# A graph layer with eleven instead of eight tiles summed from rows fetched one by one

## The chip, the cores and the metric

The kernel runs on one core of one Trainium2 chip. The metric is the device time of one execution in microseconds (us); the median of three runs before the change is 1190.65 us (1189.58 to 1191.01).

## The reference

There are N = 6250 nodes with 256 features each and E = 200,000 directed edges, sorted by destination. Every node also has an edge to itself. A graph layer comes first, then a feed-forward layer with experts; both are added to their input.

```python
x = x + gnn(layernorm(x), edge_index, W, b, prelu_a)
#   deg  = number of edges into a node (its own included); dinv = rsqrt(deg)
#   h    = x @ W
#   out  = segment_sum(h[src] * dinv[src] * dinv[dst], dst) + b
#   gnn  = where(out > 0, out, prelu_a * out)
x = x + ffn(layernorm(x)[None], Wr, br, W1, b1, W2, b2, gamma, beta)[0]
#   the mean of all rows picks 2 of 8 experts (softmax, capacity, softmax, top 2)
#   y = sum over the two of weight * (gelu(x @ W1 + b1) @ W2 + b2)
#   ffn = layernorm(y + x) * gamma + beta
```

The change lies in the segment sum: for each node, the sum of h * dinv over the sources of its edges.

## The kernel before, in words

Nodes are cut into NT = 49 tiles of 128. Each row of h * dinv is kept as two parts of reduced precision, high and low, side by side: 512 numbers, 2 KB. All 49 tiles of these rows stay in on-chip memory as `hp2`, and a copy of them goes to device memory as `hl_d` (seven stores on SP, line 786). The sum for a tile of destinations is made in one of two ways.

*Dense.* A matrix of edge counts is built, then multiplied with all rows. `one_hots` (line 605) has VectorE compare indices with a list of numbers, once for the low seven bits of the source (`oh_lo`, 128 x 2048) and once for the key that holds the source tile and which of two destinations it is (`oh_key`, 128 x 1568). `counts` (lines 639 and 643) multiplies the two, for each pair of destinations, in a matmul of 98 columns; ScalarE copies four of them at a time into the tile's count matrix `a_t`. `sums` (line 659) then runs 49 matmuls of 512 columns, one per source tile, into the accumulator `po`. A dense tile thus has 64 matmuls of 98 columns and 49 of 512.

*Gathered.* Since edges are sorted by destination, those of one tile are a contiguous piece of the edge list. The kernel takes 36 chunks of 128 edges (GC = 36). `g_edges` (line 704) fetches the piece of the source list and of the destination list, one indirect DMA each per tile, issued by GpSimd (POOL). `fetch` (line 745) issues one indirect DMA per chunk, which brings 128 rows of 2 KB from `hl_d` into one of six buffers `rows`. `g_hot` (lines 759 and 760) has ScalarE make a 128 x 128 matrix per chunk that says which edge goes to which node of the tile, and `g_sums` (lines 769 and 776) adds one matmul of 512 columns per chunk to the accumulator `pg`, after a first one for the edge to itself. `pg` has one buffer.

Eight tiles, the last ones, are gathered (NGT = 8) and 41 are dense (NDT = 41). Both kinds are done in one loop over the dense tiles, each of which is cut into four quarters (QT). Every quarter from the fifth dense tile on (G0 = 4) also holds two chunks of a gathered tile (GQ = 2), so that a gathered tile takes NQ = 18 quarters. The order on PE (TensorE), VectorE, ScalarE, SP and POOL is that of the program text in this part: it is written out by hand (`manual_schedule`), and every engine goes through its own list in order, waiting for what others must have finished. In a quarter the order in the text is: ScalarE's matrices for the chunks, the comparisons for a later quarter, the 16 count matmuls of the next tile with their copies, the 12 or 13 sums of this tile, the steps on finished tiles, and at the end the chunk matmuls and the fetches that refill the buffers they free.

Steps on finished tiles: `node` (lines 673 to 682) copies the accumulator, scales it, adds the bias, applies the slope for negative values, adds the input and stores; `stat` (lines 688 to 696) takes mean and deviation and adds to the running sum `acc` that the choice of experts is made from. `own` (line 651) adds the edge to itself to the count matrix.

`g_check` (lines 711 to 736) runs once, at the end of the third dense tile (`n == G0 - 2`). It subtracts the first node of each gathered tile from all destinations at once (line 711), counts how many fall into their tile, and compares, in a small matmul (line 724), whether the chunks held every edge; `bad_i` then says whether a slow general path is to be run. It uses a `rows` buffer as scratch and the `pg` accumulator. All sixteen list fetches stand ahead of the loop. After the loop the experts are chosen (from line 868 on, the first matmul is line 878) and the feed-forward layer runs.

Of the kernel before, what the change touches and what calls it, by code (L numbers as in the profile page):

```python
# [24 lines left out]
P = 128  # L25
# [9 lines left out]
def gnn_moe_kernel(  # L35
# [59 lines left out]
    QT = 4  # L95
    GC = 36
    GE = GC * P
    GQ = 2
    NQ = GC // GQ
    NGT = (NT - 5) * QT // (NQ + QT)  # L100
    NDT = NT - NGT
    G0 = NDT - 1 - NGT * NQ // QT
    assert E >= GE and GC % GQ == 0 and NQ % 2 == 0 and NQ > QT and G0 >= 4
# [483 lines left out]
    with main:  # L587
# [96 lines left out]
        def stat(n):  # L684
            x1 = x1s.pop(n)
            st = np_.tile([P, 6], F32, name="st2")
            mv = np_.tile([P, 2], F32, name="mv2")
            nc.vector.bn_stats(st, x1)
# [7 lines left out]
            nc.vector.scalar_tensor_tensor(  # L696
                acc[:r], x1[:r], rs[:r], acc[:r], op0=OP.mult, op1=OP.add
            )


        def g_edges():
            for v, t in ((src, g_src), (dst, g_dst)):
                for g in range(NGT):
                    nc.gpsimd.indirect_dma_start(
                        out=t[:, g, :], out_offset=None, in_=v.rearrange("(e o) -> e o", o=1),
                        in_offset=bass.IndirectOffsetOnAxis(ap=g_at[:, g : g + 1], axis=0),
                    )

        def g_check():

            nc.vector.scalar_tensor_tensor(
                g_neg, g_dst, -1.0, g_first.unsqueeze(2).to_broadcast([P, NGT, GC]),
                op0=OP.mult, op1=OP.add,
            )
            some = gp.tile([P, 2 * D], F32R, name="rows").bitcast(F32)[:, : NGT * GC]
            flat = g_neg.rearrange("p g c -> p (g c)")
            nc.vector.tensor_scalar(some, flat, 0.5, None, op0=OP.is_lt)
            nc.vector.scalar_tensor_tensor(
                some, flat, 0.5 - P, some, op0=OP.is_gt, op1=OP.mult
            )  # L720
            nc.vector.tensor_reduce(tot[:, 2:3], some, AX.X, OP.add)
            nc.vector.tensor_tensor(tot[:, 2:3], tot[:, 3:4], tot[:, 2:3], OP.subtract)
            pt = ps_g.tile([P, 2, D], F32, name="pg")[:, 0, :3]
            nc.tensor.matmul(pt, ones, tot[:, :3], start=True, stop=True)
# [15 lines left out]
        def fetch(n):  # L740

            for j in itertools.islice(g_put, n):
                if j < NGT * GC:
                    g_rows[j] = gp.tile([P, 2 * D], F32R, name="rows")
                    nc.gpsimd.indirect_dma_start(  # L745
                        out=g_rows[j], out_offset=None, in_=hl_d,
                        in_offset=bass.IndirectOffsetOnAxis(
                            ap=g_src[:, j // GC, j % GC : j % GC + 1], axis=0
                        ),
                    )  # L750

        def g_hot(j0):

            if not 0 <= j0 < NGT * GC:
                return
            oh = g_hots[j0] = og.tile([P, GQ, P], F32R, name="oh_g")
            for i in range(GQ):
                g, c = divmod(j0 + i, GC)
                nc.scalar.activation(oh[:, i, :], iota_f, AF.Abs, bias=g_neg[:, g, c : c + 1])  # L759
            nc.scalar.activation(oh, oh.bitcast(F32), AF.Relu, scale=-1.0, bias=1.0)  # L760

        def g_sums(j0):
            if not 0 <= j0 < NGT * GC:
                return
            n = NDT + j0 // GC
            if j0 % GC == 0:
# [7 lines left out]
            oh = g_hots.pop(j0)  # L774
            for i in range(GQ):
                nc.tensor.matmul(  # L776
                    pouts[n].rearrange("p k d -> p (k d)"), oh[:, i, :], g_rows.pop(j0 + i),
                    start=False, stop=((j0 + i) % GC == GC - 1),
                )
            fetch(GQ)  # L780

        for n in range(3):
            load(n)
# [8 lines left out]
        for n in ns:  # L792
# [8 lines left out]
            if n in (HK + 6, NT - 1):  # L801
# [4 lines left out]
                for b in range(NBH):  # L806
                    counts(0, (c + 1) * NBH + b)
                one_hots(c + 3) if c == 0 else None
        g_edges()

        assert NHG == QT
        for n in range(NDT):
            for c in range(NHG):
                q = (n - G0) * NHG + c
                g_hot(q * GQ)
# [24 lines left out]
        node(NDT - 1)  # L840
        stat(NDT - 1)
        order.close()

# [426 lines left out]
```

## Time and profile before

| | us |
|---|---|
| median of three runs | 1190.65 |
| the profiled execution | 1190.92 |
| its span | 1189.1 |
| TensorE busy | 1100.9 (93%) |
| VectorE busy | 711.5 (60%) |
| ScalarE busy | 630.9 (53%) |
| GpSimd busy | 529.1 (44%) |
| dense and gathered tiles, about 119 to 788 us of the span | 669 |

Times are measured from the start of the span. PE is TensorE, PEld its weight load, DVE VectorE, ACT ScalarE, POOL GpSimd, SP the engine that issues most of the transfers. A group line gives source line, engine, operation, what is written from what, the shape and a count, then busy time and the mean of one in ns, then the time its engine was idle ahead of it and what ended most of that. A line of an order of time gives start, duration and the same names; in brackets stands idle time ahead of it and what ended it. Matmuls overlap in the pipeline, so the time that one takes is read from the distance of starts.

### The profile page before, as it was taken

How to read it: one execution, taken by the hardware profiler on the slowest of the kernel's cores; microseconds unless marked ns; L12 is line 12 of the kernel's file. 1: busy time of each engine (PE TensorE's matmuls, PEld its weight loads, DVE VectorE, ACT ScalarE, POOL GpSimd, SP SyncE). 2: the span in 40 equal slices, each digit the busy share in tenths (PEclk: the TensorE clock that was granted, in tenths of full speed). 3: DMA queues.
4: the chain of work that ended last, by engine and by line, in shares of the span. 5: the costliest groups of instructions: out<-in, count | busy, mean ns of one | idle time of the engine just before them, and what ended most of it. 6: DMA issues, size and time to landing. Idle time of an engine off the chain costs nothing. (4 is left out here: it accounts for less than half of the span.)

```text
span 1189.1 us, 18227 instructions
## 1 busy us (share of the span) xinstructions
PE 1100.9 (93%) x6706; PEld 842.6 (71%) x6706; DVE 711.5 (60%) x1509; ACT 630.9 (53%) x1547; POOL 529.1 (44%) x526
## 2 busy tenths in 40 slices
PE   7882999999999999999999999952999999999996
PEld 5671878888888888888888888841666666666665
DVE  6759677788787887878878788653222232222222
ACT  3658446666666666666666666611333333333332
POOL 3704703555565555655556555400333333334433
PEclk9895999999999999999999999985999999999998
DMA  8708603565655656556565565504011111111000
GB/s 266 227 12 323 187 27 98 143 155 147 153 141 143 156 146 154 138 143 157 146 154 138 144 157 144 133 23 135 14 42 49 37 36 36 36 36 36 23 18 22
DMA packets 92254, 133.11 MB, mean 112 GB/s; under 512 B 8830, under 2 KB 47390, under 8 KB 92158
## 3 DMA queue, kind: packets, MB, share of 16 engines
q0 software_dynamic: 43584, 80.40, 27.6%
q1 hardware_dynamic: 45266, 49.06, 12.6%
q10 hardware_dynamic: 3308, 2.41, 0.7%
q8 instruction: 54, 0.88, 0.3%
q14 instruction: 42, 0.34, 0.1%
HBM read 104.47 MB, written 27.37 MB: 111 GB/s over the span
## 5 line engine op out<-in xcount | busy, mean ns | idle before, releaser
L659 PE MATMUL po<-hp,a_t 128*128 128x512 f32 x2009 | 504.2, 400 | 0.0
L745 POOL DMA_INDIRECT rows<-hl_d,g_src x288 | 329.2, 1143 | 299.1 <-PE pg L776 228.5
L659 PEld LDWEIGHTS po<-hp,a_t 128*128 128x128 f32 x2009 | 367.1, 189 | 72.7
L643 ACT CAST a_t<-pa 128x392 fp32r<-128x392 f32 x656 | 271.0, 501 | 206.2 <-PE pa L639 204.5
L605 DVE TENSOR_TENSOR oh_lo<-iota,loT 128x2048 bf16<-128x2048 bf16 x164 | 199.5, 1216 | 15.9 <-PE pa L639 15.9
L639 PEld LDWEIGHTS <-oh_lo 128*128 128x128 bf16 x2624 | 128.5, 99 | 68.2 <-issue 25.4
L1200 PE MATMUL p<-xT,w_sb 128*128 128x512 f32 (+1 forms) x416 | 172.6, 573 | 2.5 <-ACT hT L1204 1.8
L639 PE MATMUL pa<-oh_key,oh_lo 128*128 128x98 bf16 x2624 | 153.6, 211 | 22.9 <-DVE oh_key L605 12.3
L1218 PE MATMUL p<-w_sb,hT 128*128 128x256 f32 (+1 forms) x784 | 172.9, 381 | 0.0
L1218 PEld LDWEIGHTS p<-w_sb,hT 128*128 128x128 f32 (+1 forms) x784 | 148.5, 191 | 20.2
L605 DVE TENSOR_TENSOR oh_key<-iota,keyT 128x1568 bf16<-128x1568 bf16 x164 | 158.2, 965 | 0.0
L1200 PEld LDWEIGHTS p<-xT,w_sb 128*128 128x128 f32 x416 | 77.6, 192 | 90.9 <-issue 86.4
L1223 DVE TENSOR_TENSOR yt<-yt,p 128x256 f32<-128x256 f32 (+1 forms) x49 | 20.6, 421 | 164.3 <-PE p L1218 164.3
L1184 POOL TENSOR_TENSOR yt<-yt,b_sb 128x1024 f32<-128x1024 f32 (+1 forms) x13 | 29.1, 2242 | 184.0 <-PE px L1178 124.6
L1204 ACT ACTIVATE hT<-p,b_sb 128x512 f32<-128x512 f32 (+1 forms) x104 | 67.5, 661 | 79.0 <-PE p L1200 78.7
L759 ACT ACTIVATE oh_g<-iota_f,g_dst 128x128 fp32r<-128x128 f32 x288 | 103.8, 425 | 0.0
L776 PE MATMUL pg<-rows,oh_g 128*128 128x512 f32 x288 | 91.1, 397 | 0.0
L1228 ACT ACTIVATE rs<-rs 128x1 f32<-128x1 f32 (+1 forms) x49 | 9.9, 203 | 146.4 <-DVE rs L1227 146.4
L674 DVE TENSOR_TENSOR x<-x,po 128x256 f32<-128x256 f32 x41 | 17.3, 422 | 104.9 <-ACT x L673 104.9
L1233 POOL TENSOR_TENSOR yt<-yt,gamma_bc 128x256 f32<-128x256 f32 (+1 forms) x49 | 35.5, 725 | 90.2 <-DVE yt L1230 90.2
L760 ACT ACTIVATE oh_g<-oh_g 128x256 fp32r<-128x256 f32 x144 | 60.3, 419 | 4.5
L1173 DVE TENSOR_SCALAR yt<-xt,mean,rstd 128x256 f32<-128x256 f32 x49 | 18.8, 444 | 73.0 <-DMA xt<-x_d 72.8
(195 smaller groups left out, 863.3 us busy)
## 6 DMA issues: line engine op xcount, KB each, us to landing
hl_d<-hp SPq DMA_DIRECT2D x7, 1792.0 KB, 10.9
x_d<-x SPq DMA_DIRECT2D x49, 128.0 KB, 1.7
xt<-x_d SPq DMA_DIRECT2D x12, 512.0 KB, 3.9
out_dram<-yt SPq DMA_DIRECT2D x48, 128.0 KB, 1.7
xb<-in_x_dram SPq DMA_DIRECT2D x6, 896.0 KB, 11.9
xs<-in_x_dram SPq DMA_DIRECT2D x41, 128.0 KB, 3.4
rows<-hl_d,g_src POOLq DMA_INDIRECT x288, 3.8
w_sb<-in_L_ffn_W_dram ACTq DMA_DIRECT2D x2, 512.0 KB, 7.8
```

Source lines behind the costliest of these rows:

```text
L605: nc.vector.tensor_tensor(oh, iota2[:, :m, :].unsqueeze(1).to_broadcast([P, HG // 2, m, 2]), v[:, s].rearrange("p (q t) -> p q t", t=2).un ...
L639: nc.tensor.matmul(pa[:, i].rearrange("p j h -> p (j h)"), oh_lo[:, q, :, t], oh_key[:, q, :, t], start=True, stop=True,)
L643: nc.scalar.copy(tiles[n][:, :, b * 2 * BG : (b + 1) * 2 * BG], pa.rearrange("p i j h -> p h (i j)"),)
L659: nc.tensor.matmul(pouts[n].rearrange("p k d -> p (k d)"), tiles[n][:, g, :], hp2[g // TB][:, g % TB].rearrange("p k d -> p (k d)"), start ...
L745: nc.gpsimd.indirect_dma_start(out=g_rows[j], out_offset=None, in_=hl_d, in_offset=bass.IndirectOffsetOnAxis(ap=g_src[:, j // GC, j % GC : ...
L759: nc.scalar.activation(oh[:, i, :], iota_f, AF.Abs, bias=g_neg[:, g, c : c + 1])
L760: nc.scalar.activation(oh, oh.bitcast(F32), AF.Relu, scale=-1.0, bias=1.0)
L776: nc.tensor.matmul(pouts[n].rearrange("p k d -> p (k d)"), oh[:, i, :], g_rows.pop(j0 + i), start=False, stop=((j0 + i) % GC == GC - 1),)
L1200: nc.tensor.matmul(p1[:, :cols], w1_sb[:, e, k, f * P : (f + 1) * P], xT[:, k, :cols], start=(k == 0), stop=(k == ND - 1),)
L1204: nc.scalar.activation(hT[:, e, f, :cols], p1[:, :cols], AF.Gelu, bias=b1_sb[:, e, f : f + 1])
L1218: nc.tensor.matmul(p2[:r], hT[:, e, f, t * P : t * P + r], w2_sb[:, e, f, :], start=(e == 0 and f == 0), stop=(e == TOP_K - 1 and f == NF ...
L1233: nc.gpsimd.tensor_tensor(y, y, gamma_bc[:r], OP.mult)
```

## The change

Eleven tiles are gathered (NGT = 11) and 38 are dense (NDT = 38). A gathered tile takes 13 quarters instead of 18, and its 36 chunks are spread over them as evenly as whole numbers allow: two or three in a quarter, three at most (GM). The chunks begin with the third dense tile (G0 = 2) and end one quarter ahead of the loop's end. Only the edge lists of the first three gathered tiles are fetched ahead of the loop. Those of a later one are fetched in the second quarter of the gathered tile three before it, behind that quarter's row fetches, and the subtraction for it is done eight quarters later (`g_less`). `g_check` no longer does that subtraction, uses other scratch and another accumulator, and stands at the end of dense tile 35, counted from zero. The first six row fetches stand at the end of the second dense tile. The statistics of the last gathered tile come after the loop, behind the last `node`.

```diff
-    GQ = 2
-    NQ = GC // GQ
-    NGT = (NT - 5) * QT // (NQ + QT)
+    NQ = 13
+    NGT = (NT - 2) * QT // (NQ + QT)
     NDT = NT - NGT
-    G0 = NDT - 1 - NGT * NQ // QT
+    G0 = NDT - -(-NGT * NQ // QT)
+    GM = -(-GC // NQ)
...
-        def g_edges():
+        def g_edges(g):
+            if g >= NGT:
+                return
             for v, t in ((src, g_src), (dst, g_dst)):
...
+        def g_less(g):
+            if g >= NGT:
+                return
+            nc.vector.scalar_tensor_tensor(
+                g_neg[:, g, :], g_dst[:, g, :], -1.0,
+                g_first[:, g : g + 1].to_broadcast([P, GC]), op0=OP.mult, op1=OP.add,
+            )
 
         def g_check():
 
-            nc.vector.scalar_tensor_tensor(
-                g_neg, g_dst, -1.0, g_first.unsqueeze(2).to_broadcast([P, NGT, GC]),
-                op0=OP.mult, op1=OP.add,
-            )
-            some = gp.tile([P, 2 * D], F32R, name="rows").bitcast(F32)[:, : NGT * GC]
+            some = sp_.tile([P, D], F32, name="low").bitcast(BF16)[:, : NGT * GC]
...
-            pt = ps_g.tile([P, 2, D], F32, name="pg")[:, 0, :3]
+            pt = ps_o.tile([P, 2, D], F32, name="po")[:, 0, :3]
...
+        def g_chunks(q):
+
+            g, r = divmod(q, NQ)
+            return g, range(r * GC // NQ, (r + 1) * GC // NQ) if 0 <= g < NGT else ()
...
-            fetch(GQ)
+            fetch(len(chunks))
...
-        g_edges()
+        for g in range(3):
+            g_edges(g)
...
-                g_sums(q * GQ)
-            if n == G0 - 2:
+                g_sums(q)
+                if since == 1 and q > 0:
+                    g_edges(q // NQ + 3)
+                if since == 9 and q > 0:
+                    g_less(q // NQ + 3)
+            if n == max(G0 - 2, 1):
+                for g in range(3):
+                    g_less(g)
+                fetch(6)
+            if n == NDT - 3:
                 g_check()
-                fetch(6)
         node(NDT - 1)
+        if since < 2:
+            stat(done)
         stat(NDT - 1)
```

More of the change, by code (lines that the diff above doesn't have):

```diff
@@ L97, in gnn_moe_kernel @@
     GE = GC * P
-    GQ = 2
-    NQ = GC // GQ
-    NGT = (NT - 5) * QT // (NQ + QT)
+    NQ = 13
+    NGT = (NT - 2) * QT // (NQ + QT)
     NDT = NT - NGT
-    G0 = NDT - 1 - NGT * NQ // QT
-    assert E >= GE and GC % GQ == 0 and NQ % 2 == 0 and NQ > QT and G0 >= 4
+    G0 = NDT - -(-NGT * NQ // QT)
+    GM = -(-GC // NQ)
+    assert E >= GE and NQ > QT and G0 >= 2
     const = ctx.enter_context(tc.tile_pool(name="const", bufs=1))
@@ L698, in stat @@
             )
-        def g_edges():
+        def g_edges(g):
+            if g >= NGT:
+                return
             for v, t in ((src, g_src), (dst, g_dst)):
[L703 to L706, printed above, removed]
-                    )
-        def g_check():
-            nc.vector.scalar_tensor_tensor(
-                g_neg, g_dst, -1.0, g_first.unsqueeze(2).to_broadcast([P, NGT, GC]),
-                op0=OP.mult, op1=OP.add,
-            )
-            some = gp.tile([P, 2 * D], F32R, name="rows").bitcast(F32)[:, : NGT * GC]
+                nc.gpsimd.indirect_dma_start(
+                    out=t[:, g, :], out_offset=None, in_=v.rearrange("(e o) -> e o", o=1),
+                    in_offset=bass.IndirectOffsetOnAxis(ap=g_at[:, g : g + 1], axis=0),
+                )
[5 more added lines that the diff above has]
+                g_first[:, g : g + 1].to_broadcast([P, GC]), op0=OP.mult, op1=OP.add,
+            )
+        def g_check():
+            some = sp_.tile([P, D], F32, name="low").bitcast(BF16)[:, : NGT * GC]
             flat = g_neg.rearrange("p g c -> p (g c)")
@@ L750, in fetch, with g_hot, g_sums @@
                     )
-        def g_hot(j0):
-            if not 0 <= j0 < NGT * GC:
+        def g_chunks(q):
+            g, r = divmod(q, NQ)
+            return g, range(r * GC // NQ, (r + 1) * GC // NQ) if 0 <= g < NGT else ()
+        def g_hot(q):
+            g, chunks = g_chunks(q)
+            if not chunks:
                 return
-            oh = g_hots[j0] = og.tile([P, GQ, P], F32R, name="oh_g")
-            for i in range(GQ):
-                g, c = divmod(j0 + i, GC)
+            oh = g_hots[q] = og.tile([P, GM, P], F32R, name="oh_g")
+            for i, c in enumerate(chunks):
                 nc.scalar.activation(oh[:, i, :], iota_f, AF.Abs, bias=g_neg[:, g, c : c + 1])
+            oh = oh[:, : len(chunks), :]
             nc.scalar.activation(oh, oh.bitcast(F32), AF.Relu, scale=-1.0, bias=1.0)
-        def g_sums(j0):
-            if not 0 <= j0 < NGT * GC:
+        def g_sums(q):
+            g, chunks = g_chunks(q)
+            if not chunks:
                 return
-            n = NDT + j0 // GC
-            if j0 % GC == 0:
+            n = NDT + g
+            if chunks[0] == 0:
                 pouts[n] = ps_g.tile([P, 2, D], F32, name="pg")
@@ L773, in g_sums @@
                 )
-            oh = g_hots.pop(j0)
-            for i in range(GQ):
+            oh = g_hots.pop(q)
+            for i, c in enumerate(chunks):
                 nc.tensor.matmul(
-                    pouts[n].rearrange("p k d -> p (k d)"), oh[:, i, :], g_rows.pop(j0 + i),
-                    start=False, stop=((j0 + i) % GC == GC - 1),
+                    pouts[n].rearrange("p k d -> p (k d)"), oh[:, i, :],
+                    g_rows.pop(g * GC + c), start=False, stop=(c == GC - 1),
                 )
-            fetch(GQ)
+            fetch(len(chunks))
         for n in range(3):
@@ L814, in gnn_moe_kernel @@
                 q = (n - G0) * NHG + c
-                g_hot(q * GQ)
+                g_hot(q)
                 one_hots((n + 1) * NHG + c + 1)
```

## The prediction

> **What bounds the kernel now.** I read the 40 slices first, then TensorE's order of time in the middle, then the costliest groups, then GpSimd beside VectorE, and last the end of the graph stage. In the slices each digit is a tenth of 29.7 us:
>
> ```profile
> PE   7882999999999999999999999952999999999996
> POOL 3704703555565555655556555400333333334433
> PEclk9895999999999999999999999985999999999998
> ```
>
> From slice 6 to 25 TensorE has no gap (in the stretch 186 to 776 us its busy time is 590.0 of 590 us, clock 1.00), and GpSimd is half busy. So this stage is as long as TensorE's queue of work. TensorE's order of time gives the prices; columns are start, duration, engine, line, operation, tiles, shape, count:
>
> ```profile
> 124.06 0.91 PE L639 MATMUL pa<-oh_key,oh_lo 128*128 128x98 bf16 x16
> 124.79 3.01 PE L659 MATMUL po<-hp,a_t 128*128 128x512 f32 x12
> ...
> 138.60 0.91 PE L639 MATMUL pa<-oh_key,oh_lo 128*128 128x98 bf16 x16
> ...
> 161.04 3.23 PE L659 MATMUL po<-hp,a_t 128*128 128x512 f32 x13
> 165.85 0.38 PE L724 MATMUL pg<-tot,ones 128*128 128x3 f32 x2 [1.57 <-DVE tot L722]
> 166.09 0.91 PE L639 MATMUL pa<-oh_key,oh_lo 128*128 128x98 bf16 x16
> 166.82 4.59 PE L659 MATMUL po<-hp,a_t 128*128 128x512 f32 x12
> ```
>
> Durations overlap in the pipeline, so I take distances between starts. A dense tile without gathering lasts 138.60 - 124.06 = 14.54 us (four quarters). Starts further on give 305.98 and 322.43 us for one with eight gathered matmuls: 16.45 us. One gathered matmul is therefore (16.45 - 14.54) / 8 = 0.239 us. The last lines are the check of the edge lists (L724): TensorE idles 1.57 us, and the next twelve sums take 4.59 us instead of 3.00, because the clock was 0.5 for one window of 3.41 us. The check costs 1.57 + 1.59 = 3.2 us.
>
> The resource that the change loads is GpSimd, which issues one indirect fetch per chunk of 128 rows:
>
> ```profile
> L745 POOL DMA_INDIRECT rows<-hl_d,g_src x288 | 329.2, 1143 | 299.1 <-PE pg L776 228.5
> ...
> 306.17 0.94 POOL L745 DMA_INDIRECT rows<-hl_d,g_src  x1 [1.87 <-PE pg L776]
> 310.23 1.45 POOL L745 DMA_INDIRECT rows<-hl_d,g_src  x1 [1.66 <-PE pg L776]
> ...
> 309.91 0.96 DVE L605 TENSOR_TENSOR oh_key<-iota,keyT 128x1568 bf16<-128x1568 bf16 x1
> 310.80 0.41 DVE L688 BATCH_NORM_STATS2 st<-x 128x6 f32<-128x256 f32 x1
> ```
>
> A fetch is 0.94 us when it starts beside no one-hot comparison. The one at 310.23 starts inside L605, whose successor starts at 310.80: it is 0.51 us longer. Other long fetches fit the same way. Between two fetches lie 0.30 us. The wait on "PE pg L776" is for a free row buffer: GpSimd has been waiting for TensorE, not TensorE for GpSimd.
>
> **The change, part by part.**
> *Three dense tiles out:* 3 x 14.54 = -43.6 us on the path. Their 12 x (1.216 + 0.965) us on VectorE and 48 x 0.50 us on ScalarE lie beside it and save nothing by themselves.
> *Three gathered tiles in:* 108 matmuls at 0.239 us, and three seed matmuls at 0.23 us (185.82 to 186.05): +26.5 us.
> *The check moves* from the end of the third tile to the end of the 36th. It still needs a 0.24 us matmul, but the subtraction is taken out into eleven small pieces. In a later tile VectorE is done with its statistics at 312.9 and TensorE with the tile at 314.3, and the longer new tile adds about 0.7 us, so the four remaining steps (0.31, 0.46, 0.45, 0.16 us for 288 columns, about 1.9 us for 396) end about when TensorE arrives. I take -3.2 us; 0 if VectorE is late.
> *Start:* six list fetches instead of sixteen stand ahead. The first rows are used at about 153 us (end of tile 2's first quarter). Six lists from 114.5 at 1.49 us (row below) end at 123.4; the last store of the rows, issued at 116.7, lands 10.9 us later, at 127.6; six fetches end at 136.5. That leaves some 16 us; cost zero. The three small subtractions (about 0.15 us each) delay ScalarE's first gathered one-hots by under 1 us, covered by its 0.204 ms of idle time waiting on TensorE in this stage.
> *ScalarE and VectorE per quarter:* ScalarE 4 x 0.50 + 2.77 x 0.425 + about 0.5 = 3.7 of 4.3 us; VectorE (4 x 2.18 + 2.3 node + 1.84 statistics + 0.28) / 4 = 3.3, plus 0.3 for gathered nodes. Neither binds. If that cover went, ScalarE's 0.6 us would have to go first.
> *The end:* before, the last gathered tile's node step and statistics were done two quarters before TensorE ended. Now its node step comes in the last quarter and its statistics behind the last dense node. The old end:
>
> ```profile
> 776.36 11.28 PE L659 MATMUL po<-hp,a_t 128*128 128x512 f32 x49
> 788.09 0.42 DVE L674 TENSOR_TENSOR x<-x,po 128x256 f32<-128x256 f32 x1 [2.87 <-ACT x L673]
> 791.80 0.48 DVE L696 SCALAR_TENSOR_TENSOR acc<-x,rstd,acc 128x256 f32<-128x256 f32 x1
> 793.02 0.59 PE L878 MATMUL pm<-mrs,ones 128*128 128x1 f32 x2 [3.38 <-DVE mrs L876]
> ```
>
> A node step is 2.31 us (788.09 to 790.40), statistics 1.84 (790.44 to 792.28). The last quarter has 13 sums, 3.08 us. Copy 0.45, gathered node 2.31 and statistics of the tile before 1.84 make 4.60, so the last dense node starts 1.52 us behind TensorE's end instead of 0.45; then one more statistics step stands ahead of the routing (L878). +1.07 + 1.84 = +2.9 us, all on the path, since nothing but VectorE works there.
>
> *Rows in time: the disputed term.* From the first gathered quarter to the last, TensorE needs 143 x 3.635 + 396 x 0.239 + 11 x 0.235 = 617 us. In it GpSimd issues 396 row fetches and 16 lists, 412 in all. Prices: at least 0.94 + 0.30 = 1.24 us (511 us in all); the mean row 1.143 + 0.30 = 1.447 (596 us); the nearest row, sixteen list fetches back to back beside the dense work, 114.47 to 138.33 = 1.49 each (614 us); at worst, every start just inside a 1.2 us comparison, 2.3 us. So the queue that was half busy is 97 to 99% full.
>
> Here a rule speaks for the change. The Trainium skill, "SBUF — State Buffer", section "Who interferes with whom", infers that tensor_tensor does not stall GpSimd's descriptor writing, though it contends with GpSimd instructions that read SBUF. By the first half a fetch is 1.24 us, GpSimd has 17% to spare, no row is late and the sum below ends at 1173. The row at 310.23 says otherwise: the fetch, which reads its offsets, waits; by it the sum ends at 1178. I go by the row.
>
> Mean occupancy is not enough; I walk the queue. VectorE's four pairs of comparisons lie, from the start of a tile's second quarter, at 4.6-6.75, 6.85-8.95, 10.9-13.0 and 13.9-16.0 us. Three fetches per quarter, each waiting out the comparison it starts in, take until 3.6, 8.9, 12.9 and 17.1: just the 4.35 us of each quarter, so no lateness builds up, and three of 13 quarters have two chunks only (1.4 us slack each). A list pair adds 2.5 to 2.9 us once in 13 quarters. Say it falls behind the burst that ends at 8.9: lists until 11.3, the next burst's first two rows until 14.1, 5.4 us after its own quarter began. Rows land 2.4 us behind the fetch's end (3.8 us median from its start in the page's list of DMA issues), and the second of that burst is needed 8.2 us after: deadline 5.8. The margin is 0.4 us; for the other three places of the pair I get 0 to 0.4. A landing of 3 us (3.3 to 5.2 us are seen from the start) makes 0.2 to 1 us of stall. I take 0.6 us for each of eight pairs: +5 us, bounds 0 and 16 (2 us each).
>
> Why the bound matters: another page of it, "TensorE: Matmul & The Clock Gate", section "Why this matters for your kernels", allows idle gaps up to about 3 us. The row at 166.82 shows 1.57 us idle was enough for half clock. By the rule a 1.6 us stall costs 1.6, by the row 3.2. Stalls of 0.6 us are safe by both (a window only 67% busy at 85 us kept its clock).
>
> **Sum**, on the profiled execution's 1190.9 us (span 1189.1): -43.6 + 26.5 - 3.2 + 2.9 + 5 = -12.4, 1178.5. The median of the runs lies 0.3 lower: **1178 us**.
>
> **The rivals.**
> *Rows a little late, as above* (0.60): 1174 to 1186.
> *Rows never late* (0.12): 1173. For it: TensorE waited for no row before. Against it: the full queue.
> *GpSimd as bound throughout* (0.11): without the favourable phase a fetch meets a comparison at random, (1.05² + 0.88²) / (2 x 4.31) = 0.22 us, so 1.46 to 1.52 with VectorE's other two-input steps: 626 us, 9 more than TensorE: 1182; break-even at 1.54. The 1.49 row stands close by. A third of it lies at or above no change.
> *Slower by the list pairs* (0.13): if a pair makes TensorE idle 1.5 us in one clock window, it pays 1.6 more. 8 x 3.1 = 25 us eats the 17.4 gain: 1198. It decides from 2.2 us per pair. For it: the window at 163.7, 54% busy, lost the clock. Against: the walked margin.
> *Nothing comes of it* (0.04): the stalls happen to equal the gain.
>
> **How the numbers follow.** The measurement tells about 0.2%, 2.4 us. Faster: 0.60 + 0.12 + 0.08 = 0.80; same 0.06; slower 0.14. The range 1172 to 1190 holds the first two cases and most of the third.
>
> **What would show it.** Right: about 17.2 us per dense tile, TensorE waits on rows of a few us in all, behind the list fetches; no idle at the check; the routing matmul some 8.3 us behind the last sum; GpSimd over 90% busy in fetches and gaps. Wrong: waits on rows in most quarters, fetch means above 1.25 us, or half clock inside the stage.

## The result, and the profile after

| | before | after | ratio |
|---|---|---|---|
| median of 20 runs each, us | 1189.2 (1186.9 to 1191.6) | 1185.9 (1183.0 to 1189.2) | 0.9975 [0.9965, 0.9985] |
| profiled execution, us | 1190.92 | 1184.02 | |
| its span, us | 1189.1 | 1182.2 | |
| the loop (first dense sum to last), us | 667.7 | 659.7 | |

The changed kernel is faster by 3.3 us, which is a quarter of the 12 us that were forecast. The profiled execution of the kernel before lies 1.7 us above its median and that of the changed kernel 1.9 us below, so the profiles show 6.9 us of gain where the medians show 3.3. A later set of 14 runs gave 1185.4 us, 0.996 [0.9949, 0.997].

The loop starts with this row, in the kernel before and in the changed one:

```profile
119.94 4.27 PE L659 MATMUL po<-hp,a_t 128*128 128x512 f32 x12
119.38 4.48 PE L659 MATMUL po<-hp,a_t 128*128 128x512 f32 x12
```

The 40 slices of the changed kernel, the same rows as shown of the kernel before:

```profile
PE   6882999999999999999999999943999999999996
...
POOL 3704357777777777777777677710333333333433
...
PEclk9995999999999999999999999975999999999999
```

The loop is again full of TensorE work at full clock from slice 5 on, and GpSimd went from five tenths to seven. The half clock in slice 4 lies ahead of the loop, as in the kernel before.

TensorE's order of time over one gathered tile (start, duration, engine, line, operation, tiles, shape, count, idle time ahead):

```profile
149.96 3.00 PE L659 MATMUL po<-hp,a_t 128*128 128x512 f32 x12
...
153.50 0.91 PE L639 MATMUL pa<-oh_key,oh_lo 128*128 128x98 bf16 x16
154.23 3.01 PE L659 MATMUL po<-hp,a_t 128*128 128x512 f32 x12
157.08 0.87 PE L788 MATMUL pg<-rows,oh_g 128*128 128x512 f32 x3
...
158.53 0.71 PE L659 MATMUL po<-hp,a_t 128*128 128x512 f32 x2
...
207.37 1.40 PE L659 MATMUL po<-hp,a_t 128*128 128x512 f32 x5
```

A quarter with three chunks is 158.53 - 154.23 = 4.30 us. Thirteen quarters are 207.37 - 149.96 = 57.4 us, with one stall of 1.37 us in them; without it 56.0, where the prediction's prices give 13 x 3.635 + 36 x 0.239 + 0.235 = 56.1.

The waits inside the loop, 140 to 790 us (engine, tile and line, what was waited for; us in total, times, longest):

```profile
POOL rows L750 <- PE pg L788: 63.5, 68, 16.0
...
PEld pg L788 <- DMA rows<-hl_d,g_src: 12.6, 21, 1.8
```

and the costliest groups that answer to those of before (busy us, mean ns, idle ahead):

```profile
L750 POOL DMA_INDIRECT rows<-hl_d,g_src x396 | 454.1, 1147 | 173.8 <-issue 71.6
...
L788 PE MATMUL pg<-rows,oh_g 128*128 128x512 f32 x396 | 120.3, 403 | 5.8 <-DMA rows<-hl_d,g_src 5.7
```

Here is the new wait. TensorE's weight loads wait for rows 21 times, where before no row was late. The distances between TensorE's starts put the direct loss at about 8 us. At the same time GpSimd waits 63.5 us for free row buffers: it has time in sum, and is late at certain places.

The first such place, GpSimd, then VectorE, then TensorE, in order of time:

```profile
162.72 0.95 POOL L705 DMA_INDIRECT g_src<-in_src_dram,g_at  x1 [0.30 <-issue]
163.98 0.95 POOL L705 DMA_INDIRECT g_dst<-in_dst_dram,g_at  x1 [0.30 <-issue]
165.24 1.66 POOL L750 DMA_INDIRECT rows<-hl_d,g_src  x1 [0.30 <-issue]
167.20 0.95 POOL L750 DMA_INDIRECT rows<-hl_d,g_src  x1 [0.30 <-PE pa L639]
...
164.85 1.22 DVE L605 TENSOR_TENSOR oh_lo<-iota,loT 128x2048 bf16<-128x2048 bf16 x1
165.98 0.97 DVE L605 TENSOR_TENSOR oh_key<-iota,keyT 128x1568 bf16<-128x1568 bf16 x1
...
170.17 0.40 PE L788 MATMUL pg<-rows,oh_g 128*128 128x512 f32 x1
171.78 0.49 PE L788 MATMUL pg<-rows,oh_g 128*128 128x512 f32 x1 [1.21 <-DMA rows<-hl_d,g_src]
```

It is the row that the prediction's walk named, the second of the burst behind the list fetches. The walk counts from the start of the tile's second quarter, that is of its count matmuls (153.50), and has the row's fetch end 14.1 us later, at 167.6 us. It ended at 167.20 + 0.95 = 168.15, 0.55 later: the lists ended 0.1 us later than walked, and the two fetches took 0.4 more. The matmul that uses the row began at 171.78, 3.6 us behind the fetch's end and not 2.4. Without a wait it would have begun at 170.17 + 0.24 = 170.41. The stall of 1.37 us is therefore 1.2 from the longer way to its use and 0.55 from the fetch, less the walked margin of 0.4.

Behind three of the eight list pairs (the first, third and seventh) the longest wait comes at this place, three quarters behind the pair's own. Behind the others it comes later, up to three quarters more. The fourth pair, GpSimd and then TensorE:

```profile
335.63 0.95 POOL L705 DMA_INDIRECT g_dst<-in_dst_dram,g_at  x1 [0.30 <-issue]
...
352.25 1.07 POOL L750 DMA_INDIRECT rows<-hl_d,g_src  x1 [0.30 <-PE pg L788]
...
355.92 0.63 PE L788 MATMUL pg<-rows,oh_g 128*128 128x512 f32 x2
357.90 0.50 PE L788 MATMUL pg<-rows,oh_g 128*128 128x512 f32 x1 [1.35 <-DMA rows<-hl_d,g_src]
```

The matmul at 357.90 uses the row whose fetch starts at 352.25, 15.7 us behind the end of the pair, and starts 4.6 us behind that fetch's end. From the pair until 361.9 us no gap between GpSimd's fetches is longer than about 0.3 us: for 25 us it is behind. Behind the eight pairs it takes 11 to 41 us, seven times 25 or more, until a longer gap comes.

The check and the end of the stage, from TensorE's order of time:

```profile
746.82 0.87 PE L788 MATMUL pg<-rows,oh_g 128*128 128x512 f32 x3
747.66 0.39 PE L729 MATMUL po<-tot,ones 128*128 128x3 f32 x2
747.90 0.91 PE L639 MATMUL pa<-oh_key,oh_lo 128*128 128x98 bf16 x16
...
777.74 1.30 PE L659 MATMUL po<-hp,a_t 128*128 128x512 f32 x5
...
787.57 0.59 PE L900 MATMUL pm<-mrs,ones 128*128 128x1 f32 x2 [6.35 <-DVE mrs L898]
```

No gap stands ahead of the check (L729); before it was 1.57 us and a half clock. From the end of the last sum to the routing matmul it is 787.57 - 779.04 = 8.53 us, before 793.02 - 787.64 = 5.38: +3.15.

### The profile page after: what moved, and what is told of

Read it like the earlier page. It is cut to its first block, busy times and chain, and to the rows that moved or that the text cites. A ratio compares the mean times of both kernels' runs of the same rounds, so it can differ in the third digit from the quotient of the medians.

```text
span 1182.2 us, 18026 instructions
## 1 busy us (share of the span) xinstructions
PE 1086.5 (92%) x6478; PEld 826.4 (70%) x6478; DVE 687.0 (58%) x1492; ACT 653.6 (55%) x1606; POOL 659.0 (56%) x640
## 5 line engine op out<-in xcount | busy, mean ns | idle before, releaser
L750 POOL DMA_INDIRECT rows<-hl_d,g_src x396 | 454.1, 1147 | 173.8 <-issue 71.6
L659 PE MATMUL po<-hp,a_t 128*128 128x512 f32 x1862 | 466.8, 400 | 0.0
L659 PEld LDWEIGHTS po<-hp,a_t 128*128 128x128 f32 x1862 | 339.8, 189 | 66.9
L643 ACT CAST a_t<-pa 128x392 fp32r<-128x392 f32 x608 | 250.8, 501 | 165.5 <-PE pa L639 163.9
L605 DVE TENSOR_TENSOR oh_lo<-iota,loT 128x2048 bf16<-128x2048 bf16 x152 | 185.3, 1219 | 18.2 <-PE pa L639 18.2
L639 PE MATMUL pa<-oh_key,oh_lo 128*128 128x98 bf16 x2432 | 142.5, 211 | 24.4 <-ACT a_t L643 10.6
L769 ACT ACTIVATE oh_g<-iota_f,g_dst 128x128 fp32r<-128x128 f32 x396 | 134.7, 421 | 3.7 <-PE pg L788 2.8
L788 PE MATMUL pg<-rows,oh_g 128*128 128x512 f32 x396 | 120.3, 403 | 5.8 <-DMA rows<-hl_d,g_src 5.7
L788 PEld LDWEIGHTS pg<-rows,oh_g 128*128 128x128 f32 x396 | 74.1, 188 | 30.2 <-DMA rows<-hl_d,g_src 12.6
L771 ACT ACTIVATE oh_g<-oh_g 128x384 fp32r<-128x384 f32 (+1 forms) x143 | 71.6, 501 | 4.5
```

The costliest lines, as they stand in the source:

```text
L605: nc.vector.tensor_tensor(oh, iota2[:, :m, :].unsqueeze(1).to_broadcast([P, HG // 2, m, 2]), v[:, s].rearrange("p (q t) -> p q t", t=2).un ...
L639: nc.tensor.matmul(pa[:, i].rearrange("p j h -> p (j h)"), oh_lo[:, q, :, t], oh_key[:, q, :, t], start=True, stop=True,)
L643: nc.scalar.copy(tiles[n][:, :, b * 2 * BG : (b + 1) * 2 * BG], pa.rearrange("p i j h -> p h (i j)"),)
L659: nc.tensor.matmul(pouts[n].rearrange("p k d -> p (k d)"), tiles[n][:, g, :], hp2[g // TB][:, g % TB].rearrange("p k d -> p (k d)"), start ...
L750: nc.gpsimd.indirect_dma_start(out=g_rows[j], out_offset=None, in_=hl_d, in_offset=bass.IndirectOffsetOnAxis(ap=g_src[:, j // GC, j % GC : ...
L788: nc.tensor.matmul(pouts[n].rearrange("p k d -> p (k d)"), oh[:, i, :], g_rows.pop(g * GC + c), start=False, stop=(c == GC - 1),)
```

## The experiments

The runs fall into groups, each on one chip and beside the kernel before. In two groups, and in the comparison above, the kernel before took 1189 to 1190 us; in three others, on other chips, it took 1210 us. So each kernel is compared with the kernel before of its own group only, and the time of that one is given. In the recorded expectations, `e1_lists_ahead` and `t_ahead` name the two runs of the lists ahead of the loop.

### No row fetches: the floor

```diff
-                if j < NGT * GC:
-                    g_rows[j] = gp.tile([P, 2 * D], F32R, name="rows")
+                if j < NGT * GC and j >= 6:
+                    g_rows[j] = g_rows[j % 6, 0]
+                elif j < NGT * GC:
+                    g_rows[j] = g_rows[j, 0] = gp.tile([P, 2 * D], F32R, name="rows")
```

All row fetches but the first six are left out; every later chunk takes one of those six again.

> Leaves out: all row fetches but the first six; the gathered matmuls read those six buffers again and again. The lists are still fetched. Theory A (rows come late behind the list fetches and cost what is missing): the profile of the changed kernel shows some 8 us of waits on rows, so this runs 7 to 9 us under the changed kernel, about 1178 us, and TensorE has no wait on rows. Rival B (the sum was wrong elsewhere: TensorE's work or the end costs more than thought): within 2 us of the changed kernel, 1184 to 1187 us.

Measured: 1174.3 us against 1189.8, ratio 0.9879 [0.9862, 0.9896], more below the changed kernel than the 7 to 9 us expected. Run again later beside the changed kernel:

> All row fetches but the first six are left out (the sums take the first six rows again). Theory that the unnamed waits in the loop hang on the row traffic: none of them is left in the loop, and the ratio to the kernel before is about 0.988 on any chip; where the kernel before takes 1210 us that is 1195. Rival, that such a chip adds them whatever is fetched: the ratio is within 0.3% of the changed kernel's on that chip. Where the kernel before takes 1190 us this only repeats 1174.

> The changed kernel unedited, on whichever chip this call gets. If the kernel before takes about 1190 us here: 1186 us, ratio 0.997. If it takes about 1210 us: 1211 us, ratio 1.00, with waits in its loop for which the trace names no releaser, over 10 us in sum on TensorE.

Measured: 1173.9 us, 0.9861 [0.9839, 0.9884], and the changed kernel 1185.4, 0.996 [0.9949, 0.997]. TensorE's first and last sums without row fetches:

```profile
119.40 4.40 PE L659 MATMUL po<-hp,a_t 128*128 128x512 f32 x12
...
765.62 3.15 PE L659 MATMUL po<-hp,a_t 128*128 128x512 f32 x13
```

The loop is 649.4 us against 661.7 of the changed kernel in the same group and 667.7 of the kernel before. So the exchange of tiles is worth about what it was costed at, and 11.5 us of the median are lost to the fetching of rows. Set beside this loop quarter by quarter, the loop in the first profile of the changed kernel is 10.3 us longer, 9.7 of them in the third to the sixth quarter behind the eight list pairs; in the second it is 12.3, 11.7 of them there. A single pair costs 0.2 to 2.4 us. Whether the waits on the slower chips hang on row traffic wasn't tested, since this group met a chip of the other kind.

### The lists ahead of the loop

```diff
-        for g in range(3):
+        for g in range(5):
+            g_edges(g)
+        fetch(6)
+        for g in range(5, NGT):
             g_edges(g)
...
-                if since == 1 and q > 0:
-                    g_edges(q // NQ + 3)
...
-                fetch(6)
```

> All 22 list fetches ahead of the loop (ten, then the first six rows, then twelve), none among the rows. Theory A: waits on rows fall from 8 to 1 us, 6 to 8 us under the changed kernel, 1178 to 1180 us. Rival C (GpSimd's queue is full and rows are late all over, the lists only mark the places): 0 to 3 us under the changed kernel.

Measured: 1175.05 us against 1189.8, ratio 0.9886 [0.9869, 0.9903]. And again:

> All 22 list fetches ahead of the loop. Where the kernel before takes 1190 us: 1175, ratio 0.988. Where it takes 1210: 1209, ratio 0.999.

Measured: 1175.5 us, 0.9872 [0.9844, 0.9899], 9.9 us below the changed kernel of the same group and 1.6 above the kernel without row fetches. This second run's group of row fetches:

```profile
L750 POOL DMA_INDIRECT rows<-hl_d,g_src x396 | 452.0, 1142 | 163.8 <-issue 70.6
```

and TensorE's wait for rows in its loop:

```profile
PEld pg L788 <- DMA rows<-hl_d,g_src: 1.3, 3, 0.7
```

The fetches are as long as in the changed kernel (1142 against 1147 ns), and all but the first six still go out in the same quarters. Only the sixteen list fetches are gone from among them, and with them the waits. That settles the cause: the lists' place, at 9.9 / 8 = 1.2 us a pair. On this chip it beats both kernels.

### The two lists of a pair apart, in quarters of two chunks

```diff
-                if since == 1 and q > 0:
-                    g_edges(q // NQ + 3)
-                if since == 9 and q > 0:
+                if since == 4 and q > 0:
+                    g_edges(q // NQ + 3, (0,))
+                if since == 8 and q > 0:
+                    g_edges(q // NQ + 3, (1,))
+                if since == 12 and q > 0:
                     g_less(q // NQ + 3)
```

> The two list fetches of a tile stand apart, each in a quarter with two chunks only (the fifth and the ninth of the thirteen), same number in the loop. Theory A: one list in a quarter with 1.4 us of slack makes nothing late: 5 to 8 us under the changed kernel. Rival C: same number of fetches, same lateness, 0 to 2 us.

Measured: 1177.3 us against 1189.8, 0.9898 [0.9882, 0.9914]. The same list fetches in the loop, one at a time and where a quarter has two chunks, cost 2.3 us more than none of them among the rows. Most of the loss was not the fetches' time but two at once behind a full quarter; which of the two, the pair or the full quarter, counts for more isn't told apart.

### Two more list fetches, and a seventh row buffer

```diff
+                    for k in (1, 2):
+                        if q // NQ + 3 < NGT:
+                            nc.gpsimd.indirect_dma_start(
+                                out=g_src[:, (q // NQ - k) % NGT, :], out_offset=None,
```

> Every list pair in the loop is followed by two more list fetches into lists no longer or not yet in use. Theory A: each of eight places is 2.8 us later still, 22 us over the changed kernel, about 1208 us, and more (up to 1221 us) if the longer waits halve TensorE's clock for a window each time. If the places of the lists are not what makes rows late: under 5 us over it.

Measured: 1236.3 us against 1210.6, 1.0241 [1.0201, 1.028].

> Two more list fetches (of the same two lists again) behind each pair, eight times. Theory that each fetch among the rows delays the rows behind it and nothing takes the delay up: 2 more fetches of 1.25 us on GpSimd, eight times, is 20 us over the changed kernel, and more where a stall halves the clock: 1205 to 1216 where the kernel before takes 1190. Rival, that the first pair's cost is a matter of its place and the slack takes up the rest: under 1195.

Measured: 1239.2 against 1209.9, 1.0275 [1.021, 1.0341]. Against the unedited changed kernel on a chip of that kind (1210.9, below) that is 25 to 28 us for sixteen fetches. The second run's waits in the loop:

```profile
PE pg L788 <- DMA rows<-hl_d,g_src: 17.8, 15, 2.2
...
PEld pg L788 <- DMA rows<-hl_d,g_src: 11.8, 10, 1.8
```

and its granted clock in the 40 slices:

```profile
PEclk9896899999999989999989999995899999999998
```

TensorE's own waits for rows are 17.8 us (5.4 in the unedited kernel on such a chip), and the clock digits fall inside the loop, where the granted clock was 0.5 for nine windows of 3.4 us in seven places (the unedited kernel on such a chip has one). Five of the seven stand right behind waits on rows, each of two pieces that come to 2.2 to 3.7 us; one stands behind 2.3 us on ScalarE's matrix and 0.6 on a row, one behind 3.9 us on VectorE. This is the rival that the prediction called slower by the list pairs, with half clock.

```diff
-        gp = main.enter_context(tc.tile_pool(name="gp", bufs=6))
+        gp = main.enter_context(tc.tile_pool(name="gp", bufs=7))
...
-            xs[n] = np_.tile([P, D], F32, name=name, bufs=3 if name == "xs" else 1)
+            xs[n] = np_.tile([P, D], F32, name=name, bufs=2 if name == "xs" else 1)
```

> The changed kernel with seven row buffers instead of six, lists still among the rows (room for it: two buffers for the input rows and one for a scratch tile instead of three and two). A row then has a third of a quarter, 1.4 us, more time. Theory A (a deadline missed by about 1 us behind each list pair): 7 to 10 us under the changed kernel, 1176 to 1179 us. Rival C (GpSimd's throughput): within 3 us of the changed kernel.

> Seven row buffers instead of six, paid for with one buffer less of two other small tiles. Theory that single rows come late behind the list fetches: a seventh row ahead gives about 1.6 us more (one chunk of the gathered tile: 57.4 / 36), which is more than most stalls seen, so most of the 10 us come back: 1175 to 1178 where the kernel before takes 1190. Rival, that GpSimd has too little time through the whole of the loop: the same as the changed kernel, 1184 to 1186. Where the kernel before takes 1210 us: 1210, and nothing is told apart.

Measured: 1211.7 (0.9994 [0.9971, 1.0017]) and 1208.5 (0.9996 [0.9976, 1.0015]), both where the kernel before takes 1210 us. In time nothing is told apart. In the trace of the second, the wait for rows is almost gone (in that of the first, TensorE has none):

```profile
PEld pg L788 <- DMA rows<-hl_d,g_src: 0.8, 2, 0.4
```

The unedited kernel on such a chip waits 10.3 us on the same line. One row more in flight removes the lateness, as a late burst would have it and a GpSimd short of time would not. What it is worth where the kernel before takes 1190 us wasn't measured.

### Without comparisons: what lengthens a fetch

```diff
+            if u > 1:
+                ohs[u] = ohs[u % 2]
+                return
```

All one-hot comparisons but the first two pairs are left out; the counts are made from those two again.

> Leaves out: all one-hot comparisons but the first two pairs, which the count matmuls then read throughout. If the comparisons are what makes a fetch longer, the mean of a row fetch falls from 1.147 us to 0.95 us, no row is late, and the waits on late comparisons (2 us) go too: 8 to 11 us under the changed kernel, 1175 to 1178 us. If tensor_tensor does not hold GpSimd up, fetches stay near 1.15 us and rows stay late: within 3 us of the changed kernel.

Measured: 1169.9 us against 1189.8, 0.9842 [0.9827, 0.9857]. TensorE never waits for a row, its weight loads do for 0.5 us in all. The row fetches:

```profile
L753 POOL DMA_INDIRECT rows<-hl_d,g_src x396 | 373.8, 944 | 243.5 <-PE pg L791 142.4
```

Without the comparisons the mean fetch is 944 ns, the same as one that starts beside none, and 203 ns shorter than in the changed kernel. So a fetch is held up by VectorE's running two-input comparison, as the row at 310.23 said, and the inference of the Trainium skill, "SBUF — State Buffer", section "Who interferes with whom", that tensor_tensor doesn't stall descriptor writing, does not carry over to these fetches as a whole. They also read their offsets, and the same section says that such an operation contends with GpSimd's reads; which of the two is held up, no run tells. The time is 4.4 us under the kernel without row fetches. Its loop is 2.6 us shorter, 2.2 of them the late comparisons (below), and starts 2.2 us earlier.

### The end of the stage

```diff
                 if since == 0 and NDT <= done < NT:
                     node(done)
+                    if q == NGT * NQ:
+                        stat(done)
...
-                if c == 3 and n > 0:
+                if c == (3 if n < NDT - 1 else 2) and n > 0:
                     stat(n - 1)
...
-        if since < 2:
-            stat(done)
```

This is put on top of the lists ahead.

> Lists ahead of the loop as in e1_lists_ahead, and a shorter end: the statistics of the tile before the last dense one a quarter earlier, those of the last gathered tile directly behind its node step. VectorE then has 0.45 + 2.3 + 1.8 us ahead of the last dense node against 3.1 us of sums, so it starts about 1.1 us late and one node and one statistics step remain: if the end costs what the chain says, 2 us under e1_lists_ahead, about 1173 us. If the routing behind it waits for something else, no difference.

Measured: 1207.6 against 1210.6, 0.9981 [0.9959, 1.0002].

> Lists ahead, and the statistics of the tile before the last moved one quarter ahead and those of the last tile right behind it. The stretch from the last sum to the mean's product shrinks from 8.5 to 6.5 us, so the theory that the end is a chain of statistics expects 2 us below t_ahead: 1173 where the kernel before takes 1190. Rival, that the time saved is given back by a later step of the end: the same as t_ahead.

Measured: 1174.5 against 1189.8, 0.9871 [0.9847, 0.9894]; lists ahead alone 1175.5 in the same group. TensorE at the end of the stage, in the second run:

```profile
769.74 1.29 PE L659 MATMUL po<-hp,a_t 128*128 128x512 f32 x5
...
777.55 0.58 PE L900 MATMUL pm<-mrs,ones 128*128 128x1 f32 x2 [4.25 <-DVE mrs L898]
```

From the last sum's end to the routing matmul it is 777.55 - 771.03 = 6.52 us, 2.0 less than the 8.53 of the lists ahead alone. The mechanism is there in the trace; the medians, 1.0 us apart, don't tell it from nothing.

### The check alone

The kernel before, with only its check moved to the end of the third tile from the last and its scratch and accumulator exchanged.

```diff
-            some = gp.tile([P, 2 * D], F32R, name="rows").bitcast(F32)[:, : NGT * GC]
+
+        def g_check2():
+
+            some = sp_.tile([P, D], F32, name="low").bitcast(BF16)[:, : NGT * GC]
...
+            if n == NDT - 3:
+                g_check2()
```

> The kernel before, with the check alone moved to the end of tile NDT - 3 and the subtraction left where it was. Expected from the gap and the half clock behind it: 3.2 us under the kernel before. If the gap is paid elsewhere: no difference.

Measured: 1209.7 against 1210.6, 0.9996 [0.9987, 1.0004]. Its repetition is among the next runs. Nothing is gained, against the 3.2 us expected. But on these chips TensorE stands still elsewhere at that time (next rows), so this doesn't measure the 3.2 us; they stay a reading of the two traces.

### The same kernels where the kernel before takes 1210 us

> The changed kernel again, unedited, as the reference for the runs beside it: on an occasion on which the kernel before takes about 1190 us, 1186 us (ratio 0.9975). In the second group of runs the kernel before took 1211 us and showed waits for nothing that the profile names; if this group is like that one, theory D (instructions arrive late when the row traffic is dense) expects a ratio of 0.999 or more, with such waits inside the loop.

> Lists ahead of the loop, again, beside the changed kernel: ratio to the kernel before 0.9886 as in the first group, 11 us under the changed kernel, if the occasion is like the first; if it is like the second, 5 to 11 us under the changed kernel.

> Lists ahead and the shorter end, now beside the lists ahead alone: 2 us under it, as worked out from the chain at the end (6.5 instead of 8.5 us from the last sum to the routing matmul). No difference if something else holds the routing.

> The kernel before with the check alone moved: 3.2 us under the kernel before (1.57 us of gap and 1.59 us of half clock); no difference if the gap is paid elsewhere.

Measured, against 1209.6: the changed kernel 1210.9, 1.002 [1.0004, 1.0036]; lists ahead 1209.8, 0.9987 [0.9968, 1.0006]; with the end 1208.7, 0.9983 [0.9963, 1.0003]; the check alone 1209.6, 1.0 [0.9992, 1.0008]. Moving the check is worth nothing here, within 1 us, and the changed kernel is no faster. The 1.2% of the lists ahead isn't there either. What is different: in the kernel before with its check moved, TensorE and VectorE stand still early in the loop for what the trace gives no releaser. The first row is TensorE's, the second VectorE's; "issue" marks a wait for nothing that the trace shows, "remote" one ended by a signal whose sender it doesn't show:

```profile
154.46 0.48 PE L639 MATMUL pa<-oh_key,oh_lo 128*128 128x98 bf16 x4 [5.43 <-issue]
...
154.79 1.23 DVE L605 TENSOR_TENSOR oh_lo<-iota,loT 128x2048 bf16<-128x2048 bf16 x1 [10.05 <-remote]
```

In the changed kernel such waits lie scattered over the whole loop. VectorE's waits in it:

```profile
DVE rstd L694 <- issue: 10.8, 11, 3.2
DVE x L674 <- issue: 9.6, 3, 3.8
...
DVE oh_lo L605 <- remote: 1.0, 1, 1.0
```

Where the kernel before takes 1190 us, VectorE's list of waits has no such entry for the changed kernel. The loop is 677.2 us for the changed kernel (661.7 there), 679.7 with the lists ahead (650.1 there), and 679.4 for the kernel before with its check moved, where the kernel before has 667.7. So every kernel loses some 12 us or more in its loop, and the lists ahead lose most, 29.5 us. Of these, 19 are more idle time of TensorE (20.9 us against 1.7), and about 8.5 are the clock: it was 0.5 for 17.1 us of that loop, 13.7 of them at one stretch from 158.5 us on, among such waits. In the kernel before with its check moved TensorE idles 9.4 us, and half clock for 13.7 us costs about another 6.8. A guess that instructions are brought late while rows are moved densely would fit waits of several engines at once; but packets on the instruction queues took no longer there (0.70 us in the mean for the changed kernel against 0.72), which speaks against it. What these waits are stays open.

## Why the prediction was right or wrong

The sum again, with what the two profiled executions and the runs give for each step:

| step | forecast, us | found, us | from |
|---|---|---|---|
| tiles exchanged | -17.1 | -17.3 | loop without row fetches 649.36 against 667.70, less the steps two and four of this table |
| check | -3.2 | -3.2 | read: no gap and full clock at 747.66 |
| end | +2.9 | +3.15 | 8.53 against 5.38 |
| VectorE in the loop | 0 | +2.2 | late comparisons, also in the kernel without row fetches |
| rows late | +5 | +10.3 | loop 659.66 against 649.36 |
| around it | 0 | -2.0 | loop starts 0.5 us earlier, 1.5 less behind the routing matmul |
| sum | -12.4 | -6.9 | profiled executions 1190.9 and 1184.0 |

The first row is what is left when the second is taken as read; only their sum, -20.5, is measured. The medians lie at -3.3 and -4.4, because the two profiled executions lie on opposite sides of theirs. A second profiled execution of the changed kernel (1183.9 us) has a loop of 661.7 us, two more than the first, so that its rows cost 12.3. Of the -2.0 us around the loop, 1.5 lie behind the routing matmul, which the change doesn't touch, and the start of the loop differs by 1.8 us between the two executions of the changed kernel (119.4 and 117.6 us): that part of the gain is luck.

**The step that failed** is the one on rows: "I take 0.6 us for each of eight pairs: +5 us". The wait was right: rows come late behind the list pairs, and the lateness of one pair is gone before the next. The size was off by a factor of two, 1.2 to 1.5 us for a pair in the mean. Its bounds, 0 to 2 us, held that. Two things in it fell short.

What was mis-sized most is "Rows land 2.4 us behind the fetch's end". That is a median, and counts to the row's landing; a landing of 3 us was allowed for when 0.6 was taken. In the changed kernel the last packet comes 2.5 us behind the fetch's end in the median too, but up to 4.0 for single rows (2.74 for the row shown, at 170.88), and the matmul starts up to 0.9 us after it; the weight load waits with it. Over the five longest waits the way from the fetch's end to the use was 2.8 to 4.6 us, and the walked margins of 0 to 0.4 us are gone. An estimate from the same rows: had each been usable at 2.4 us, about 1.4 of the 8 us of direct waits would be left. Why single rows take so long isn't shown. The kernel before couldn't show it directly: its nearest use of a row was 7.3 us behind the fetch's end. In the changed kernel 34 of 396 rows are used less than 3.6 us behind it.

The other is the walk's reach. It followed one burst behind the pair, where its end for the second row was 0.55 us early, and held that no lateness builds up beyond it. There stands the longest wait of three pairs of eight. Behind the others GpSimd stayed behind, and a slow row met it up to three quarters later (the matmul at 357.90).

**"Neither binds"**, said of VectorE and ScalarE from the mean of a quarter (3.3 of 4.3 us), failed in five quarters. VectorE and the TensorE matmul that waits for it:

```profile
209.00 0.42 DVE L674 TENSOR_TENSOR x<-x,pg 128x256 f32<-128x256 f32 x1 [3.58 <-ACT x L673]
...
211.24 0.41 DVE L674 TENSOR_TENSOR x<-x,po 128x256 f32<-128x256 f32 x1
...
214.60 0.97 DVE L605 TENSOR_TENSOR oh_key<-iota,keyT 128x1568 bf16<-128x1568 bf16 x1
...
215.63 0.91 PE L639 MATMUL pa<-oh_key,oh_lo 128*128 128x98 bf16 x16 [0.26 <-DVE oh_key L605]
```

A gathered and a dense node step (each 2.3 us) stand back to back in one quarter, the comparisons behind them come late, and TensorE loses 0.4 us. Three such places, and two where a gathered tile's statistics stand behind a dense node step, are the 2.2 us.

**The rule against the row.** The forecast took the row at 310.23 over the rule that a comparison does not stall descriptor writing, and the kernel without comparisons shows that the fetch as a whole is stalled (944 against 1147 ns). For the clock it took the row at 166.82 over the Trainium skill, "TensorE: Matmul & The Clock Gate", section "Why this matters for your kernels", which allows idle gaps of up to about 3 us. Single waits of up to 1.5 us in the changed kernel's loop didn't cost the clock. Longer ones went both ways; the first of these two rows, from the first run with four lists, was followed by half clock, the second, from the kernel with its lists apart, was not:

```profile
448.40 0.50 PE L788 MATMUL pg<-rows,oh_g 128*128 128x512 f32 x1 [1.57 <-DMA rows<-hl_d,g_src]
768.79 0.50 PE L788 MATMUL pg<-rows,oh_g 128*128 128x512 f32 x1 [1.69 <-DMA rows<-hl_d,g_src]
```

The traces can be set in order by how busy TensorE was in the window of 3.41 us. Over the loops of all twenty, each of the 26 windows at full clock in which it was under 48% busy was followed by half clock, and none over 54% was; of six between 50 and 54%, among them the 54% at 163.7 us and the windows of the two rows above (both 50%), three were. So half a window of idle time in these loops is where the clock goes, whether in one piece or two. It is no general bound: ahead of the loop, a window 78% busy (at 74.9 us in the kernel before) was followed by half clock.

**The rivals.** *Never late* was the floor: 1173 forecast, 1174 measured without row fetches, 1175 with the lists ahead. *GpSimd as bound throughout* falls, though its 1182 us is nearer than my own number, by luck: GpSimd waited 63.5 us for free buffers, and with the same 396 fetches, as long as before, the lists ahead came to the floor. *Slower by the list pairs* gave its break-even at 2.2 us for a pair; on the chips with 1190 us it was 1.2 to 1.5, and with four lists it happened. *Nothing comes of it* is what the other chips show, but for a reason that no case named.

## What to carry to other kernels

A prefetch's lead time runs from the end of its issue to the start of the first instruction that uses the data, weight load and release included; time the nearest use, not the last packet, before working with margins of tenths of a microsecond. When a queue is nearly full, one more pair of instructions costs what it delays behind it, so place it where the queue has room (one at a time, or ahead of the loop), which was worth two to three times the change itself here, on the one kind of chip. A queue that only just keeps up stays behind for long: walk it until it has caught up (here up to 41 us), not for one burst. Mean occupancy of a period says nothing of the one quarter in which two steps meet; walk each engine through the fullest quarter.

## What the hardware showed that was not expected

- The kernel before takes 1190 us on one chip and 1210 us in the median on three others. Most of the 20 us are a loop that starts 8 us later and is 12 us longer, with waits early in it for which the trace names no releaser (read from the kernel before with its check moved). With dense row fetching such waits spread over the loop, and the spread of the runs grows (the changed kernel 1204.5 to 1219.6 us). A gain of 1.2% on the one chip was 0.1% on another, which its interval doesn't tell from none.
- A fetch that reads its offsets on GpSimd takes 0.944 us in the mean with no comparison about and 1.12 to 1.16 us among them.
- No row was used earlier than 2.35 us behind the end of its fetch in any trace, and at the waits of the changed kernel it was 2.6 to 4.6 us.
